# A selective-scan layer on one Trainium2 core: the copy of dt*u one group sooner, other buffer counts, and halo copies on another engine

## The chip, the core and the metric

The kernel runs on one core of a Trainium2 chip. A core has TensorE (PE in the profile; PEld is its weight load), VectorE (DVE), ScalarE (ACT), GpSimd (POOL), and SyncE (SP), which issues most of the transfers. Each engine works through its own queue of instructions in order, and engines wait for each other through semaphores. SBUF is the working memory on the chip, PSUM the memory that TensorE writes. The metric is the time of one execution on the device in microseconds (us), here the median of three.

## What is computed

The reference has two layers. Layer 1 of the program (a fractional Fourier block) is not touched. Layer 2 is a state-space block on a tensor of 4 images, 192 channels and 128 x 128 positions, read as sequences of 16,384 positions:

```python
seq = (seq - mu) * rsqrt(var + eps) * ln_g + ln_b        # over 192 channels
xs, z = split(seq @ in_proj_w.T)                         # 384 channels each
u = silu(causal_conv4(xs) + conv_b)
dt, B, C = split(u @ x_proj_w.T)                         # ranks 12, 16, 16
dt = softplus(dt @ dt_proj_w.T + dt_proj_b)
# for each channel d, state s and position t
h[d,s,t] = h[d,s,t-1] * exp(dt[d,t] * A[d,s]) + (dt[d,t] * u[d,t]) * B[s,t]
y[d,t] = sum_s h[d,s,t] * C[s,t] + u[d,t] * Dp[d]
out = x + (y * silu(z)) @ out_proj_w.T
```

A group normalisation of x stands before each layer, and its statistics for layer 2 come out of layer 1.

## The kernel before

Layer 2 is the function layer1 (the code counts from zero). Positions are cut into chunks of T = 512: 32 per image, 128 in all, numbered n. The 384 channels are three tiles of 128, numbered j. The 16 states are taken in eight groups of G = 2, numbered sg. So a chunk has 24 groups, k = 8j + sg, and the main loop has 3072 positions, pos. The order of the instructions is written out by hand (a manual schedule): each engine executes its instructions in the order in which the loop emits them.

A group's own work is spread over several positions:

- inputs (L747 to L756), emitted two groups ahead: db, the product of dt\*u with B. For sg = 1, 4, 7 GpSimd computes it from SBUF (L752). For the other five VectorE does (L754), and reads dt\*u from dp, a copy in PSUM that ScalarE makes once per j (dtu_copy, L740 to L744; one buffer).
- decay (L767): da = exp(dt\*A) on ScalarE into one of three PSUM buffers, three scans ahead. Each decay is emitted right behind the scan that frees its buffer.
- scans (L769 to L791): two scans h on VectorE (L780), each followed by a decay; between the two a callable named between is called; after them the carry copy on ScalarE (L787), and the product hc of h and C on GpSimd (L789). h has three buffers.
- sums (L792), LAG = 3 groups later: eight TensorE transposes of hc that add up into py (L802); py has one PSUM buffer.
- once per j: evacuate, a ScalarE copy of py (L811) at sg = 3; turn on TensorE at sg = 4 (L817, L819); gate on VectorE at sg = 5 (L827).

Between these pieces runs front, a generator that prepares the chunk after next: at every position the loop takes one step of it. It goes through the channel normalisation (L603 to L648), the input projection (L654), the xs activations (L667), the convolution (L672), two Silu steps (L680, L684; each loads another activation table and then the one for exp again), the projection px (L710), its copy xd, which goes to HBM as dbc and comes back broadcast as bc (L735), Softplus (L726), and dt\*u (L730, GpSimd). A front starts at k = 18 of chunk n for chunk n+2 and ends at k = 20 of chunk n+1. Where it yields LATE, the part after the yield is emitted in the same position, but behind the scans. In its middle lies this chain, one step per position: sum of squares (PE), square root (ACT), reciprocal (DVE, L634, late at k = 0), transpose into rt (PE, L637, k = 1), rows (ACT, L640, late at k = 1), broadcast by four selecting matmuls (PE, L644, k = 2), and s \*= that (DVE, L648, late at k = 2). The first input projection follows at k = 3. All of the front's and the turn's PSUM tiles are one pool, ps, of three buffers. finish (L829 to L846) is a generator, too: it projects a whole chunk back (L836, at k = 8 and 9 of the next chunk) and adds the residual on VectorE (L841, late).

The convolution reaches three positions back. A chunk's first three columns of xs are copied from halo (L663), and its last three are copied into halo (L668), both on GpSimd.

In the loop body the order of emission is: a step of finish; turn; sums of the group three back; dtu_copy for the group two on, if that begins a new j (sg = 6); at sg = 3 of every j the evacuation, which is handed to scans as the callable between, except at k = 19, where Softplus comes and the evacuation is emitted ahead of it; a step of the front; inputs; gate; scans; the late parts.

Of the kernel before, what the change touches and what calls it, by code (L numbers as in the profile page):

```python
# [10 lines left out]
F32 = mybir.dt.float32  # L11
# [18 lines left out]
T = 512  # L30
# [11 lines left out]
def _bc(ap, axis, n):  # L42

    a = ap.unsqueeze(axis)
    shape = list(a.shape)
    shape[axis] = n
    return a.to_broadcast(shape)
# [455 lines left out]
def layer1(tc, xmid, out, st2, w, n_tok=S * S):  # L503

    nc = tc.nc
    B = len(xmid)
    NCHUNK = n_tok // T
    G = 2
    LAG, FRONT, BCL = 3, 18, 5
    SOFTPLUS = 19  # L510
    LATE = True
    with ExitStack() as ctx:
        def pool(name, bufs, **kw):
            return ctx.enter_context(tc.tile_pool(name=name, bufs=bufs, **kw))
# [8 lines left out]
        scp = pool("l1s", 4)  # L523
# [53 lines left out]
        halo = cp.tile([128, NJ, 3], F32, name="halo")  # L577
# [6 lines left out]
        NG = NS // G  # L584
# [3 lines left out]
        def load_x(i):  # L588
            b, ch = divmod(i, NCHUNK)
            xm = xp.tile([CH, 2, T], F32, name="xm")  # L590
            nc.sync.dma_start(
                out=xm, in_=xmid[b][:, ch * T : (ch + 1) * T].rearrange("(t p) f -> p t f", p=CH)
            )
            got[i]["xm"] = xm

        def front(i):
# [15 lines left out]
            yield  # L612
            yield LATE
            nc.vector.scalar_tensor_tensor(
# [17 lines left out]
            nc.scalar.activation(rs, var[:, 0:4], AF.Sqrt, bias=eps, scale=1.0 / C)  # L632
            yield LATE
            nc.vector.reciprocal(rs, rs)  # L634
            yield
            rt = psum()
            nc.tensor.transpose(rt[0:4, 0:128], rs, ident)  # L637
            yield LATE
            rows = tp.tile([4, 128], F32, name="rows")
            nc.scalar.copy(rows, rt[0:4, 0:128])  # L640
            yield
# [1 line left out]
            for q in range(4):  # L643
                nc.tensor.matmul(  # L644
                    rb[0:CH, q * 128 : (q + 1) * 128], sel[:, q, :], rows, start=True, stop=True
                )
            yield LATE
            nc.vector.tensor_tensor(s, s, _bc(rb[0:CH], 1, 2), ALU.mult)  # L648
# [10 lines left out]
            xs = lp.tile([128, NJ, T + 3], F32, name="xs")  # L659
            if ch == 0:  # L660
                nc.gpsimd.memset(xs[:, :, 0:3], 0.0)
            else:
                nc.gpsimd.tensor_copy(xs[:, :, 0:3], halo)  # L663
            for j in range(NJ):
                pp = in_proj(j)
                yield
                nc.scalar.activation(xs[:, j, 3:], pp, AF.Identity, bias=bxz[:, j : j + 1])  # L667
            nc.gpsimd.tensor_copy(halo, xs[:, :, T : T + 3])  # L668

            def conv(j, pc, half):  # L670
                for k in (2 * half, 2 * half + 1):
# [60 lines left out]
        def load_bc(i, sg):  # L732

            t = bcp.tile([128, 2, G, T], F32, name="bc")
            nc.sync.dma_start(  # L735
                out=t, in_=got[i]["dbc"][:, sg * G : (sg + 1) * G, :].partition_broadcast(128)
            )
            got[i]["bc", sg] = t

        def dtu_copy(n, j):  # L740

            g = got[n]
            g["dp"] = psd.tile([128, T], F32, name="dp")
            nc.scalar.copy(g["dp"], g["dtu"][j])  # L744

        def inputs(n, k):

            g = got[n]
            j, sg = divmod(k, NG)
            db = scp.tile([128, G, T], F32, name="db")  # L750
            if sg in (1, 4, 7):
                nc.gpsimd.tensor_tensor(db, _bc(g["dtu"][j], 1, G), g["bc", sg][:, 0], ALU.mult)  # L752
            else:
                nc.vector.tensor_tensor(db, _bc(g["dp"], 1, G), g["bc", sg][:, 0], ALU.mult)  # L754
            g["db", k] = db
# [4 lines left out]
        def decay(at):  # L760

            if at < len(states):
                n, k, q = states[at]
                j, sg = divmod(k, NG)
                st = sg * G + q
                das[at] = psa.tile([128, T], F32, name="da")
                nc.scalar.activation(das[at], got[n]["dt"][j], AF.Exp, scale=A[:, j, st : st + 1])  # L767

        def scans(pos, n, k, between):  # L769
            g = got[n]  # L770
            j, sg = divmod(k, NG)
            ch = n % NCHUNK
            if k == 0:
                g["carry"] = tp.tile([128, NJ, NS], F32, name="carry")
                g["before"], last["carry"] = last.get("carry"), g["carry"]
            db = g.pop(("db", k))
            h = scp.tile([128, G, T], F32, name="h", bufs=3)
            for q in range(G):
                st = sg * G + q
                nc.vector.tensor_tensor_scan(  # L780
                    h[:, q, :], das.pop(G * pos + q), db[:, q, :],
                    0.0 if ch == 0 else g["before"][:, j, st : st + 1], ALU.mult, ALU.add,
                )
                decay(G * pos + q + 3)
                if q == 0:
                    between()
            nc.scalar.copy(g["carry"][:, j, sg * G : (sg + 1) * G], h[:, :, T - 1])  # L787
            hc = scp.tile([128, G, T], F32, name="hc")
            nc.gpsimd.tensor_tensor(hc, h, g["bc", sg][:, 1], ALU.mult)  # L789
            g["hc", k] = hc  # L790

# [16 lines left out]
        def evacuate(n, j):  # L808
            g = got[n]
            yt = g["yt", j] = op.tile([128, T // 128, 128], F32, name="yt")  # L810
            nc.scalar.copy(yt, g["py", j])  # L811
# [17 lines left out]
        def finish(n):  # L829
# [3 lines left out]
            for t in range(2):  # L833
                po = psum()
                for j in range(NJ):
# [3 lines left out]
                    )  # L839
                yield LATE  # L840
                nc.vector.tensor_add(xm[:, t, :], po[0:CH], xm[:, t, :])  # L841
# [7 lines left out]
        order = [(n, k) for n in range(total) for k in range(NGR)]  # L849
        fronts = []  # L850
# [2 lines left out]
            if n < total:  # L853
                fronts.append(front(n))

        def step(works):

            late = []
            for f in list(works):
                got_on = next(f, f)  # L860
                if got_on is f:
                    works.remove(f)
                elif got_on is LATE:
                    late.append(f)
            return late

        with tc.manual_schedule():
            for i in range(min(2, total)):
                load_x(i)
            for _ in front(0):  # L870
                pass
            for sg in range(NG):
                load_bc(0, sg)
            dtu_copy(0, 0)
            for pos in range(2):
                inputs(*order[pos])
            for at in range(3):
                decay(at)


            start_front(1)
            for _ in range(NGR - FRONT):
                for f in step(fronts):
                    next(f)
            tails = []
            for pos, (n, k) in enumerate(order):
                j, sg = divmod(k, NG)
                if k == FRONT:
                    start_front(n + 2)
                if k == NGR - 3 and n + 1 < total:  # L890
                    assert len(fronts) == (n + 2 < total), fronts
                late = step(tails)
                if pos >= NG and sg == LAG + 1:
                    turn(*before)
                if pos >= LAG and sg != LAG:
                    sums(*order[pos - LAG])
                if sg == NG - 2 and pos + 2 < len(order):
                    m, q = order[pos + 2]
                    dtu_copy(m, q // NG)
                if pos >= NG and sg == LAG:  # L900

                    before = n - (j == 0), (j - 1) % NJ
                    if k == SOFTPLUS:
                        evacuate(*before)
                late += step(fronts)
                if pos + 2 < len(order):
                    inputs(*order[pos + 2])
                if pos >= NG and sg == LAG + 2:
                    gate(*before)
                if pos >= NG and sg == LAG and k != SOFTPLUS:  # L910
                    scans(pos, n, k, lambda: evacuate(*before))
                else:
                    scans(pos, n, k, lambda: None)
                for f in late:
                    next(f, None)
                if pos >= LAG and sg == LAG:
                    sums(*order[pos - LAG])
                if k == NG - 1 and n:
                    tails.append(finish(n - 1))
                if k == FRONT - 6 and n + 2 < total:  # L920
                    load_x(n + 2)
                if k >= NGR - BCL and n + 1 < total:
                    load_bc(n + 1, k - (NGR - BCL))
                if k < NG - BCL and n:
                    load_bc(n, k + BCL)
            for at in order[-LAG:]:
                sums(*at)
            evacuate(total - 1, NJ - 1)
            turn(total - 1, NJ - 1)
            gate(total - 1, NJ - 1)  # L930
            for _ in finish(total - 1):
                pass
# [139 lines left out]
```

## Time and profile before

The time is 12446.84 us, median of three runs (12438.11 to 12448.03). The profiled run took 12437.32 us; its span is 12435.5 us. Layer 2 begins near 1500 us and fills the rest.

| engine | busy us | share of the span |
|---|---|---|
| PE (matmul) | 10160.7 | 82% |
| DVE | 11004.8 | 88% |
| ACT | 8226.0 | 66% |
| POOL | 10446.5 | 84% |

| group of instructions | count | mean ns of one |
|---|---|---|
| L789 POOL hc, 128x1024 | 3072 | 2358 |
| L752 POOL db, 128x1024 | 1152 | 2394 |
| L730 POOL dt\*u, 128x512 | 384 | 1277 |
| L780 DVE h, 128x512 | 5952 | 1263 |
| L754 DVE db, 128x1024 | 1920 | 1203 |
| L767 ACT da, 128x512 | 6144 | 688 |
| L787 ACT carry, 128x2 | 3072 | 177 |

A group's busy time is a sum over instructions, and consecutive instructions of one engine overlap a little, so the distance between their starts is shorter than their mean. In a timeline each row is a run of like instructions: start, duration of the run, engine, line, operation, operands, count, and, in brackets, how long the engine had been idle before it and what ended that wait. In the view of the waits a row is: the engine and the instruction that waited, what it waited for, the total, how many times, and the longest. Where an instruction waits for several others, the row names the one that came last by the trace, which may be another one that ended at about the same time.

### The profile page before, as it was taken

The numbers are of one execution on the slowest core, as the hardware profiler recorded it, in microseconds if no ns is written. First come the engines' busy times: TensorE is split into PE (matmuls) and PEld (weight loads), VectorE is DVE, ScalarE is ACT, GpSimd is POOL, SyncE is SP. The second block draws the span as 40 slices with busy tenths as digits, with TensorE's granted clock in tenths as the row PEclk, the third lists the DMA queues.
The fourth block names the chain that finished last, engine by engine and source line by source line (L and its number), as shares of the span: only waits on it lengthen the run. The fifth ranks groups of instructions, "written<-read, shape, count | busy, mean of one in ns | idle before, by whom it ended". The sixth has DMA issues, their size and how long they took to land.

```text
span 12435.5 us, 128056 instructions
## 1 busy us (share of the span) xinstructions
PE 10160.7 (82%) x43146; PEld 6339.5 (51%) x43146; DVE 11004.8 (88%) x10176; ACT 8226.0 (66%) x14055; POOL 10446.5 (84%) x4978
## 2 busy tenths in 40 slices
PE   4778888888888888888888888888888888888887
PEld 2434455555555555555555555555555555555554
DVE  5566599999999999999999999999999999999998
ACT  2322277777777777777777777777777777777776
POOL 0000299999999999999999999999999999999999
PEclk8888688888888888888888888888888888888888
DMA  8787532332332332332333323323323323333232
GB/s 214 210 218 200 149 117 105 107 117 97 115 117 93 117 116 96 117 110 102 117 105 107 117 98 114 117 93 117 116 96 117 111 101 117 106 106 117 98 114 89
DMA packets 503659, 1489.12 MB, mean 120 GB/s; under 512 B 67889, under 2 KB 118774, under 8 KB 502486
## 3 DMA queue, kind: packets, MB, share of 16 engines
q1 hardware_dynamic: 482518, 1418.00, 34.8%
q0 software_dynamic: 13312, 50.34, 1.3%
q10 hardware_dynamic: 7168, 12.59, 0.3%
q8 instruction: 340, 5.57, 0.2%
q14 instruction: 321, 2.63, 0.1%
HBM read 1325.19 MB, written 155.32 MB: 119 GB/s over the span
## 4 chain that ended last, share of the span: by engine, by line
DVE 47%; PE 19%; ACT 19%; issue 12%; POOL 2%; DMA 2%; SPq 0%; POOLq 0%; ACTq 0%; DVEq 0%
DVE h L780 32%; DVE db L754 11%; PE ps L654 6%; ACT da L767 6%; PE py L802 3%; ACT L767 3%; PE ps L644 2%; ACT dt L726 2%; PE pr L470 2%; ACT dp L744 1%; ACT L680 1%; ACT u L680 1%; DVE s L648 1%; ACT L726 1%; PE ps L722 1%
## 5 line engine op out<-in xcount | busy, mean ns | idle before, releaser
L789 POOL TENSOR_TENSOR hc<-h,bc 128x1024 f32<-128x1024 f32 x3072 | 7200.2, 2358 | 576.2 <-DVE h L780 415.3
L780 DVE TENSOR_TENSOR_SCAN h<-da,carry,db 128x512 f32<-128x512 f32 x5952 | 7246.0, 1263 | 218.1 <-ACT da L767 218.1
L767 ACT ACTIVATE da<-dt,c_A_log 128x512 f32<-128x512 f32 x6144 | 4171.0, 688 | 2832.5 <-DVE h L780 2815.7
L802 PE MATMUL py<-ident,hc 128*128 128x128 f32 x24576 | 3815.5, 309 | 1308.6 <-POOL hc L789 1019.8
L802 PEld LDWEIGHTS py<-ident,hc 128*128 128x128 f32 x24576 | 3320.1, 161 | 2586.0 <-issue 1363.4
L752 POOL TENSOR_TENSOR db<-dtu,bc 128x1024 f32<-128x1024 f32 x1152 | 2757.3, 2394 | 5.3 <-DMA bc<-dbc 5.3
L754 DVE TENSOR_TENSOR db<-dp,bc 128x1024 f32<-128x1024 f32 x1920 | 2310.5, 1203 | 482.3 <-ACT dp L744 445.8
L654 PE MATMUL ps<-s,c_wiT 96*128 96x512 f32 x3072 | 1689.1, 678 | 167.6 <-DVE s L648 167.6
L672 PE MATMUL ps<-xs,dcw 128*128 128x512 f32 x3072 | 1436.9, 597 | 18.0 <-ACT zs L684 0.5
L654 PEld LDWEIGHTS ps<-s,c_wiT 96*128 96x128 f32 x3072 | 586.1, 212 | 655.7 <-issue 443.6
L767 ACT ACT_TABLE_LOAD x636 | 816.0, 1283 | 11.3
L672 PEld LDWEIGHTS ps<-xs,dcw 128*128 128x128 f32 x3072 | 532.0, 190 | 480.0 <-issue 432.5
L476 POOL DMA_DIRECT2D xmid<-xt x64 | 42.6, 666 | 785.2 <-DVE xt L474 778.5
L836 PE MATMUL ps<-yg,c_woT 128*96 128x512 f32 x1536 | 700.8, 592 | 0.0
L787 ACT COPY carry<-h 128x2 f32<-128x2 f32 x3072 | 543.3, 177 | 2.6 <-DVE h L780 2.6
L817 PE MATMUL ps<-u,ddp 128*128 128x512 f32 x768 | 532.1, 782 | 0.0
L730 POOL TENSOR_TENSOR dtu<-dt,u 128x512 f32<-128x512 f32 x384 | 478.5, 1277 | 19.8 <-ACT dt L726 19.8
L191 DVE BATCH_NORM_STATS2 st<-xt 96x6 f32<-96x512 f32 x512 | 322.1, 677 | 155.3 <-DMA xt<-in_x 154.0
L836 PEld LDWEIGHTS ps<-yg,c_woT 128*96 128x96 f32 x1536 | 250.1, 163 | 400.9 <-issue 371.1
L710 PE MATMUL ps<-u,c_xpT 128*128 128x512 f32 x768 | 442.3, 719 | 0.0
L667 ACT ACTIVATE xs<-ps,bxz 128x512 f32<-128x512 f32 x384 | 264.6, 689 | 213.6 <-PE ps L654 198.9
L474 DVE TENSOR_TENSOR xt<-xt,pr 96x1024 f32<-96x1024 f32 x128 | 154.1, 1212 | 275.2 <-PE pr L470 208.8
(162 smaller groups left out, 8368.9 us busy)
## 6 DMA issues: line engine op xcount, KB each, us to landing
bc<-dbc SPq DMA_DIRECT2D x1024, 1024.0 KB, 6.7
xt<-in_x SPq DMA_DIRECT2D x192, 768.0 KB, 8.6
xmid<-xt POOLq DMA_DIRECT2D x64, 768.0 KB, 7.2
xm<-xmid SPq DMA_DIRECT2D x128, 384.0 KB, 3.3
out<-xm SPq DMA_DIRECT2D x128, 384.0 KB, 3.0
d<-x ACTq DMA_DIRECT2D x64, 192.0 KB, 7.5
df<-u SPq DMA_DIRECT2D x16, 512.0 KB, 5.0
u<-df SPq DMA_DIRECT2D x16, 512.0 KB, 11.8
```

What stands on the lines that cost most here:

```text
L654: nc.tensor.matmul(pp, wiT[:, t, m * 128 : (m + 1) * 128], s[:, t, :], start=t == 0, stop=t == 1)
L672: nc.tensor.matmul(pc, dcw[:, j, k, :], xs[:, j, k : k + T], start=k == 0, stop=k == 3)
L730: nc.gpsimd.tensor_tensor(dtu[j], dt[j], u[j], ALU.mult)
L752: nc.gpsimd.tensor_tensor(db, _bc(g["dtu"][j], 1, G), g["bc", sg][:, 0], ALU.mult)
L754: nc.vector.tensor_tensor(db, _bc(g["dp"], 1, G), g["bc", sg][:, 0], ALU.mult)
L767: nc.scalar.activation(das[at], got[n]["dt"][j], AF.Exp, scale=A[:, j, st : st + 1])
L780: nc.vector.tensor_tensor_scan(h[:, q, :], das.pop(G * pos + q), db[:, q, :], 0.0 if ch == 0 else g["before"][:, j, st : st + 1], ALU.mult ...
L787: nc.scalar.copy(g["carry"][:, j, sg * G : (sg + 1) * G], h[:, :, T - 1])
L789: nc.gpsimd.tensor_tensor(hc, h, g["bc", sg][:, 1], ALU.mult)
L802: nc.tensor.matmul(py[:, blk, :], hc[:, q, blk * 128 : (blk + 1) * 128], ident, start=first, stop=sg == NG - 1 and q == G - 1 and blk == T ...
L817: nc.tensor.matmul(pf, ddp[:, j, :], g["u"][j], start=True, stop=True)
L836: nc.tensor.matmul(po[0:CH], woT[:, j, t * CH : (t + 1) * CH], g["yg", j], start=j == 0, stop=j == NJ - 1,)
```

## The change

Four edits, all in layer 2:

1. The copy of dt\*u into dp is emitted one group sooner, at sg = 5 instead of 6. Within a chunk it stands ahead of the front's step; for the first j of the next chunk it is emitted between the two scans.
2. The rows of 1/std are copied from PSUM between the two scans of their position (that is, between two decays in ScalarE's queue) and not behind the scans.
3. The products hc have five buffers instead of four, the products db three instead of four.
4. The two halo copies go from GpSimd to ScalarE.

The purpose of 1 and 2 is to have an operand of VectorE ready sooner, of 3 to let TensorE lag further behind GpSimd at the same use of SBUF, of 4 to take work off GpSimd.

```diff
-            yield LATE
+            yield MID
             rows = tp.tile([4, 128], F32, name="rows")
             nc.scalar.copy(rows, rt[0:4, 0:128])
...
-                nc.gpsimd.tensor_copy(xs[:, :, 0:3], halo)
+                nc.scalar.copy(xs[:, :, 0:3], halo)
...
-            nc.gpsimd.tensor_copy(halo, xs[:, :, T : T + 3])
+            nc.scalar.copy(halo, xs[:, :, T : T + 3])
...
-            db = scp.tile([128, G, T], F32, name="db")
+            db = scp.tile([128, G, T], F32, name="db", bufs=3)
...
-            hc = scp.tile([128, G, T], F32, name="hc")
+            hc = scp.tile([128, G, T], F32, name="hc", bufs=5)
...
-                if sg == NG - 2 and pos + 2 < len(order):
-                    m, q = order[pos + 2]
-                    dtu_copy(m, q // NG)
-                if pos >= NG and sg == LAG:
-
+
+                new = order[pos + 3] if sg == NG - 3 and pos + 3 < len(order) else None
+                if new and new[1]:
+                    dtu_copy(new[0], new[1] // NG)
+                    new = None
+
+                done = pos >= NG and sg == LAG
+                if done:
                     before = n - (j == 0), (j - 1) % NJ
                     if k == SOFTPLUS:
                         evacuate(*before)
-                late += step(fronts)
+                        done = False
+                step(fronts, parts)
...
-                if pos >= NG and sg == LAG and k != SOFTPLUS:
-                    scans(pos, n, k, lambda: evacuate(*before))
-                else:
-                    scans(pos, n, k, lambda: None)
-                for f in late:
-                    next(f, None)
+
+                def between():
+                    if done:
+                        evacuate(*before)
+                    if new:
+                        dtu_copy(new[0], 0)
+                    go_on(parts[MID])
+
+                scans(pos, n, k, between)
+                go_on(parts[LATE])
```

More of the change, by code (lines that the diff above doesn't have):

```diff
@@ L510, in layer1 @@
     SOFTPLUS = 19
-    LATE = True
+    MID, LATE = "mid", "late"
     with ExitStack() as ctx:
@@ L854, in start_front, with step @@
                 fronts.append(front(n))
-        def step(works):
-            late = []
+        def step(works, parts):
             for f in list(works):
@@ L862, in step, with go_on @@
                     works.remove(f)
-                elif got_on is LATE:
-                    late.append(f)
-            return late
+                elif got_on is not None:
+                    parts[got_on].append(f)
+        def go_on(fs):
+            for f in fs:
+                next(f, None)
         with tc.manual_schedule():
@@ L882, in layer1 @@
             for _ in range(NGR - FRONT):
-                for f in step(fronts):
-                    next(f)
+                parts = {MID: [], LATE: []}
+                step(fronts, parts)
+                go_on(parts[MID] + parts[LATE])
             tails = []
@@ L891, in layer1 @@
                     assert len(fronts) == (n + 2 < total), fronts
-                late = step(tails)
+                parts = {MID: [], LATE: []}
+                step(tails, parts)
                 if pos >= NG and sg == LAG + 1:
@@ L904, in layer1 @@
                         evacuate(*before)
-                late += step(fronts)
+                        done = False
+                step(fronts, parts)
                 if pos + 2 < len(order):
```

## The prediction

> **What bounds the kernel now.** I read the busy time of the steady part first, then the waits of VectorE and GpSimd, then the timelines of DVE, POOL and PE over one chunk. Numbers k = 0..23 are the groups of a chunk; E(k) is the end of its scans on DVE, H(k) the end of its hc product on POOL. Busy time per engine over 10,000 us of layer 2 (columns: stretch, length, busy and count per engine, granted clock, DMA share, GB/s):
>
> ```profile
> 2000.00:12000.00 10000.00, 8325.53 (x36455) 5292.90 (x36453) 9290.78 (x8322) 7207.74 (x12423) 9475.54 (x4455) 0.86 0.32 109
> ```
>
> No engine is full, and two are close: POOL 94.8%, DVE 92.9%. One chunk takes 85.33 us: the normalisation L648 starts at 6032.27 and, 35 chunks later, at 9018.93, and 2986.66 / 35 = 85.333. So per chunk DVE works 79.3 and waits 6.05; POOL works 80.9 and waits 4.5. The waits of DVE, then of POOL, in the same stretch (117 chunks; total, times, longest):
>
> ```profile
> DVE db L754 <- ACT dp L744: 408.6, 352, 2.2
> DVE h L780 <- ACT da L767: 211.3, 235, 1.9
> DVE s L648 <- PE ps L644: 88.5, 117, 0.9
> ```
> ```profile
> POOL hc L789 <- DVE h L780: 373.9, 459, 1.3
> POOL hc L789 <- PE py L802: 146.5, 118, 2.0
> ```
>
> Per chunk DVE waits 3.5 us for the copy of dt*u, 1.8 for decays, 0.76 for the 1/std rows. The change aims at the first and third. What will they uncover? The DVE timeline of one chunk (start, us, engine, line, ..., idle before in brackets), at k = 2 to 3, 6, 9 and 14:
>
> ```profile
> 6032.27 1.22 DVE L648 TENSOR_TENSOR s<-s,ps 96x1024 f32<-96x1024 f32 x1 [0.76 <-PE ps L644]
> ...
> 6045.27 1.22 DVE L754 TENSOR_TENSOR db<-dp,bc 128x1024 f32<-128x1024 f32 x1 [1.86 <-ACT dp L744]
> ...
> 6058.70 0.69 DVE L841 TENSOR_TENSOR xm<-ps,xm 96x512 f32<-96x512 f32 x1
> ...
> 6073.33 1.22 DVE L754 TENSOR_TENSOR db<-dp,bc 128x1024 f32<-128x1024 f32 x1 [1.36 <-ACT dp L744]
> ```
>
> The PE timeline, from the last sums of the old chunk to the second output projection:
>
> ```profile
> 6028.04 1.90 PE L802 MATMUL py<-ident,hc 128*128 128x128 f32 x8 [1.93 <-POOL hc L789]
> 6030.22 2.02 PE L644 MATMUL ps<-rows,sel 4*96 4x128 f32 x8 [0.28 <-ACT rows L640]
> 6033.55 3.78 PE L654 MATMUL ps<-s,c_wiT 96*128 96x512 f32 x4 [1.31 <-DVE s L648]
> ...
> 6055.93 2.74 PE L836 MATMUL ps<-yg,c_woT 128*96 128x512 f32 x6
> 6058.50 1.04 PE L802 MATMUL py<-ident,hc 128*128 128x128 f32 x8
> ```
>
> Two things are to be seen. From 6033.55 PE shows no idle time to speak of until 6077.4: it is the busy engine of that stretch although it is at 83% overall. And L836 ends at 6055.93 + 2.74 = 6058.67, when the DVE addition that reads it starts at 6058.70 just as its scans end: no wait is recorded there, but there is no slack either. Last, POOL:
>
> ```profile
> 6025.61 6.99 POOL L789 TENSOR_TENSOR hc<-h,bc 128x1024 f32<-128x1024 f32 x3
> ...
> 6068.89 2.36 POOL L789 TENSOR_TENSOR hc<-h,bc 128x1024 f32<-128x1024 f32 x1 [0.58 <-DVE h L780]
> 6071.21 2.41 POOL L752 TENSOR_TENSOR db<-dtu,bc 128x1024 f32<-128x1024 f32 x1
> 6073.58 2.36 POOL L789 TENSOR_TENSOR hc<-h,bc 128x1024 f32<-128x1024 f32 x1
> 6077.09 2.34 POOL L789 TENSOR_TENSOR hc<-h,bc 128x1024 f32<-128x1024 f32 x1 [1.15 <-DVE h L780]
> ```
>
> After 6077.09 (k = 14) POOL never waits until the next chunk's k = 4: it is behind DVE there, and hc(23), the first of the three at 6025.61, ends at 6027.94, 5.9 us after its scans.
>
> [...] four input-projection matmuls take 3.78 us at 6033.55 and 1.88 later. [...]
>
> **The change part by part** (time 0 is the start of L648, trace 6032.27).
>
> *dt\*u copy sooner, k = 5.* ACT copies right after carry(4), ahead of the xs activation that waits for PE until 10.5. It is done near 9.5, and DVE's db at E(5) = 11.03 no longer waits: −1.86, and some 0.08 of scan start-up that each idle gap costs (a pair of scans is 2.36 start to start, 2.45 alone). DVE's own work after E(5) is 3.48 (db 1.12 and scans), 2.36, 3.48, 4.08 (with an addition of 0.6) for k = 6 to 9, so it could be at E(9) at 24.4 instead of 26.43. But L836 is at the end of PE's unbroken run, which starts 1.28 after L648. Only PE's one gap in it can close: the conv at 6054.11 waits about 0.3 for the z buffers that ACT frees, and ACT is 2 us earlier now. So L836 ends at 26.1, DVE waits about 0.5 at the first addition and 1.2 at the second, and its lead over the kernel before is 26.43 − 26.1 = 0.3 us. Of 1.94, 0.3 is left.
>
> *k = 13.* The copy comes after carry(12), while ACT is catching up with the two Silu table loads: the copy ends at 39.27, the scans at E(13) = 39.3. Wait gone, at most 0.05 left. E(14) falls from 44.6 to 42.8. POOL, which idled 1.15 before hc(14), now runs hc(12), db, hc(13), hc(14) without a gap: hc(14) starts at 43.30 instead of 44.82 (0.33 + 1.15 earlier), and from there POOL sets the pace to H(23), 36.2 us on: 79.5.
>
> *k = 21, next chunk.* The copy sits between the two scans; dtu[0] is ready at H(19) + 1.25 = 63.1 and ACT gets there at 64.9. The 0.25 us wait goes, but DVE isn't the late one there: nothing.
>
> *1/std rows between two decays.* In the trace the copy starts at 6029.92, behind the second decay; the first decay of that group ends at 6028.72, and the copy would start there, 1.2 us sooner. But the matmuls L644 also stand behind the sums of hc(23) in PE's queue, so they can't start before H(23) + 0.1 + 1.90. In the trace: 6029.98 instead of 6030.22. Gain 0.25; the L648 wait doesn't vanish. After the change L648 starts at H(23) + 4.06 (0.1, 1.90, 2.02, two hand-overs) = 79.5 + 4.06 = 83.55, whereas DVE is there at 82.5: from E(14) to E(23) it takes 30.5 today, 30.3 without the 0.25 wait at k = 22, so E(23) = 73.1, and 9.4 more to E(2) (6022.06 to 6031.45): its wait grows from 0.76 to about 1.05.
>
> *Buffers.* POOL's wait for PE py, 1.25 per chunk, is hc(6) at 6049.00. The scans of group 6 end at 6048.78, and every hc that waits for scans starts 0.22 to 0.25 after them (6068.64 to 6068.89). So the scans release it; sums(2), which frees the buffer, ended at 6043.6. A fifth buffer for C products buys nothing. Three for B products cost nothing: db(k+2) on POOL follows hc(k−1), which had waited for scans(k−1) anyway, and DVE follows itself.
>
> *Halo copies.* POOL loses two copies of 0.15 us start to start, both before a wait for DVE (hc(4), hc(6)): nothing. ACT gains two; [...] the carry copy of 2 measures 177. They lie after xs activations; the decay behind the second is ready at 14.5 and wanted at 15.7. Hidden under ACT's waits for DVE (2560.7 us in the same stretch, 21.9 per chunk). They add no foreign wait.
>
> **Sum.** Per chunk 0.3 (what PE leaves of k = 6) + 1.2 (k = 14, through POOL) + 0.25 (rows) = 1.77; 85.33 → 83.55. Times 127 chunk distances = 225 us; 12446.84 − 225 = 12222. [...] I take 12225.
>
> **Rivals.** (1) *The waits simply vanish.* For it: they are on DVE, the first engine in the chain of waits at 47%. DVE's period would be 85.33 − 3.5 − 0.76 − 0.4 (start-ups) = 80.7, POOL's floor 80.9 − 0.3 = 80.6: 81 us, 11,900. Against: L836 without slack, sums(23) ahead of L644. A half form, where [...] the k = 9 wait disappears, gives 82: 12,020. (2) *PE keeps the period.* [...] 85.33, about 12,447. [...] (3) *ACT becomes the late one.* The rows copy now waits for a PE transpose with a decay behind it, and the k = 21 copy waits for POOL. If POOL's lag eats the slack (2.5 and 1.8 us), decays are late and DVE and POOL wait: 0.6 us per chunk gives 12,525. Against: those slacks.
>
> **How the numbers follow.** Main case 0.69 (83.2 to 84.2: 12,180 to 12,310); rival 1 with its half form 0.18; rival 2 0.06; rival 3 0.07. The range from 12,030 to 12,330 holds the main case and the half form, and leaves out the full form, 2 and 3. Faster by over 0.2% is the main case and rival 1: 0.87; same 0.06; slower 0.07.
>
> **What would show it.** DVE waits for dp gone; new waits of xm L841 for PE L836 of some 1.5 us per chunk; the wait of L648 at about 1 rather than 0.76, released by PE with PE waiting for hc before it; POOL's py wait relabelled or gone, its halo copies gone; the wait for a decay at k = 20 unchanged at 1.6. No wait at L841 would make me wrong toward 11,900; waits of decays behind rows or dp toward slower.

## The result, and the profile after

The changed kernel takes 12333.99 us (median of four runs, 12330.82 to 12339.48), against 12446.15 for the kernel before: a ratio of 0.9912, with a 95% interval of 0.9894 to 0.9929. It is faster by under 1%, clear of the noise, and by about half of what was forecast (12225); the time lies 4 us above the upper end of the forecast range (12,330).

The steady part of layer 2, as a busy time per engine over 10,000 us of the kernel after (stretch, length, busy and count for PE, PEld, DVE, ACT, POOL, granted clock, DMA share, GB/s):

```profile
2000.00:12000.00 10000.00, 8362.49 (x36805) 5238.58 (x36806) 9526.04 (x8407) 7321.74 (x12786) 9540.85 (x4267) 0.84 0.32 111
```

DVE is at 95.3% now, where it was at 92.9%. The chunk period has fallen from 85.33 to 84.45 us (from the first to the last start of L730, over 127 chunks: 1506.0 to 12231.1, against 1491.1 to 12327.5). That is 0.88 less per chunk, 112 us in all. In this pair of profiled runs about 15 us go the other way before layer 2 starts (the first L730 is at 1506.0 instead of 1491.1). That part of the code is not touched by the change, and in the traces of the experiments below the first L730 lies anywhere from 1492 to 1505; the cause of this shift is open.

The waits of DVE in the kernel after, in the same stretch (119 chunks), and then those of POOL:

```profile
DVE h L780 <- ACT da L767: 156.1, 122, 1.6
DVE xm L841 <- PE ps L836: 128.7, 206, 1.1
DVE s L648 <- PE ps L644: 74.5, 118, 1.3
DVE yg L827 <- PE ps L819: 42.6, 63, 0.8
```
```profile
POOL hc L789 <- DVE h L780: 372.5, 415, 1.6
POOL hc L789 <- PE py L802: 29.7, 31, 1.2
POOL hc L789 <- PE ps L819: 24.5, 26, 1.0
```

POOL still waits 3.1 us per chunk for DVE's scans (372.5 / 119); what is left of its waits for PE is 0.25 for the sums py and 0.2 for the projection. POOL follows DVE, as before.

All of the 408.6 us of waits for dp are gone, and two new waits have come: the additions L841 wait 1.1 us per chunk for PE's projection, and the gates L827 0.36 for PE's turn. So far this is the forecast. But the waits of DVE have fallen from 6.05 to 3.4 us per chunk, by 2.65, and the period by 0.88 only. DVE's busy time has grown by 1.2 us per chunk (9526 x 84.45 / 10,000 = 80.4 against 79.3) although it executes the same instructions. The remaining 0.6 are gaps too short for the list of waits. Where do the two come from? The timeline of DVE has the answer. First a pair of scans and the db behind it in the kernel before, then in the kernel after (start, duration, engine, line):

```profile
6004.27 2.45 DVE L780 TENSOR_TENSOR_SCAN h<-da,carry,db 128x512 f32<-128x512 f32 x2
6006.64 1.20 DVE L754 TENSOR_TENSOR db<-dp,bc 128x1024 f32<-128x1024 f32 x1
```
```profile
6057.85 2.45 DVE L780 TENSOR_TENSOR_SCAN h<-da,carry,db 128x512 f32<-128x512 f32 x2
6060.34 1.23 DVE L754 TENSOR_TENSOR db<-dp,bc 128x1024 f32<-128x1024 f32 x1
```

Before, db starts 2.37 us after the scans start, that is, 0.08 before they end: the two overlap. After, it starts 2.49 after, 0.04 behind their end, and it takes 1.23 instead of 1.20. Each db that directly follows scans (11 of 15 in a chunk) now costs 0.12 to 0.15 us more.

Is it the scans that db waits for, or does db no longer overlap anything? A db with the small reciprocal L634 between it and the scans tells, in the kernel after:

```profile
6076.41 2.45 DVE L780 TENSOR_TENSOR_SCAN h<-da,carry,db 128x512 f32<-128x512 f32 x2
6078.78 0.15 DVE L634 RECIPROCAL rs<-rs 128x4 f32<-128x4 f32 x1
6078.89 1.22 DVE L754 TENSOR_TENSOR db<-dp,bc 128x1024 f32<-128x1024 f32 x1
```

The scans end at 6078.86, and db starts 0.03 behind that, while the reciprocal still runs until 6078.93. So it is the end of the scans that holds it.

The same view, the rows of the new waits in one chunk of the kernel after:

```profile
6012.66 1.23 DVE L754 TENSOR_TENSOR db<-dp,bc 128x1024 f32<-128x1024 f32 x1
...
6022.45 0.69 DVE L841 TENSOR_TENSOR xm<-ps,xm 96x512 f32<-96x512 f32 x1 [0.23 <-PE ps L836]
...
6027.62 0.69 DVE L841 TENSOR_TENSOR xm<-ps,xm 96x512 f32<-96x512 f32 x1 [0.98 <-PE ps L836]
```

At k = 6 db doesn't wait for dp any more, and 10 and 15 us later the additions wait for L836. And PE, around the rows of 1/std in the next chunk:

```profile
6081.51 1.97 PE L802 MATMUL py<-ident,hc 128*128 128x128 f32 x8 [2.06 <-POOL hc L789]
6083.41 2.02 PE L644 MATMUL ps<-rows,sel 4*96 4x128 f32 x8
6086.74 3.78 PE L654 MATMUL ps<-s,c_wiT 96*128 96x512 f32 x4 [1.31 <-DVE s L648]
```

L644 no longer waits for the rows (0.28 us before). It follows the sums of hc(23) without a gap, and these wait for POOL, as forecast.

### The profile page after: what moved, and what is told of

It reads as the page before. It is cut to its first block, busy times and chain, and to the rows that moved or that the text cites. A ratio compares the mean times of both kernels' runs of the same rounds, so it can differ in the third digit from the quotient of the medians.

```text
span 12337.7 us, 127805 instructions
## 1 busy us (share of the span) xinstructions
PE 10127.7 (82%) x43146; PEld 6238.7 (51%) x43146; DVE 11156.9 (90%) x10176; ACT 8268.8 (67%) x14307; POOL 10410.8 (84%) x4726
## 5 line engine op out<-in xcount | busy, mean ns | idle before, releaser
L802 PE MATMUL py<-ident,hc 128*128 128x128 f32 x24576 | 3764.4, 306 | 1277.1 <-POOL hc L789 1034.1
L802 PEld LDWEIGHTS py<-ident,hc 128*128 128x128 f32 x24576 | 3228.3, 159 | 2659.2 <-POOL hc L789 1448.0
L754 DVE TENSOR_TENSOR db<-dp,bc 128x1024 f32<-128x1024 f32 x1920 | 2346.3, 1222 | 105.4 <-DMA bc<-dbc 37.2
L654 PE MATMUL ps<-s,c_wiT 96*128 96x512 f32 x3072 | 1688.9, 678 | 167.8 <-DVE s L648 167.8
L654 PEld LDWEIGHTS ps<-s,c_wiT 96*128 96x128 f32 x3072 | 586.0, 212 | 655.7 <-issue 443.2
L836 PE MATMUL ps<-yg,c_woT 128*96 128x512 f32 x1536 | 700.8, 592 | 0.0
L817 PE MATMUL ps<-u,ddp 128*128 128x512 f32 x768 | 587.5, 858 | 0.0
L730 POOL TENSOR_TENSOR dtu<-dt,u 128x512 f32<-128x512 f32 x384 | 478.4, 1276 | 54.8 <-ACT dt L726 54.8
L836 PEld LDWEIGHTS ps<-yg,c_woT 128*96 128x96 f32 x1536 | 249.9, 163 | 401.0 <-issue 399.3
L722 PE MATMUL ps<-xd,c_dtT 12*128 12x512 f32 x768 | 198.2, 856 | 307.9 <-ACT xd L713 307.9
```

Source lines behind the costliest of these rows:

```text
L654: nc.tensor.matmul(pp, wiT[:, t, m * 128 : (m + 1) * 128], s[:, t, :], start=t == 0, stop=t == 1)
L730: nc.gpsimd.tensor_tensor(dtu[j], dt[j], u[j], ALU.mult)
L802: nc.tensor.matmul(py[:, blk, :], hc[:, q, blk * 128 : (blk + 1) * 128], ident, start=first, stop=sg == NG - 1 and q == G - 1 and blk == T ...
L817: nc.tensor.matmul(pf, ddp[:, j, :], g["u"][j], start=True, stop=True)
L836: nc.tensor.matmul(po[0:CH], woT[:, j, t * CH : (t + 1) * CH], g["yg", j], start=j == 0, stop=j == NJ - 1,)
```

## The experiments

The theory after this reading is A: the third B buffer makes the shortfall. With three buffers db(k+2) overwrites the buffer of db(k−1), which the scans of group k−1, the instruction right ahead of it in DVE's own queue, have just read; so it waits for their end. With four it overwrites db(k−2), which was read a group earlier. The rivals for the shortfall: B, PE's switch to full clock (a granted clock of 0.50, then 1.00; its times stand under the chunk periods) comes later on average after the change; C, the fifth C buffer matters. ("C buffers" are those of hc, "B buffers" those of db.)

### x1: four buffers each, the other three edits kept

```diff
-            db = scp.tile([128, G, T], F32, name="db", bufs=3)
+            db = scp.tile([128, G, T], F32, name="db")
-            hc = scp.tile([128, G, T], F32, name="hc", bufs=5)
+            hc = scp.tile([128, G, T], F32, name="hc")
```

> The changed kernel with four buffers each for the C products and the B products again; its other three edits stay. Theory A (the shortfall is the third B buffer: with three, the db that follows the scans of group k-1 overwrites the db those scans read, so DVE waits for its own scans to end, 0.13 us start to start at each of some 12 db per chunk): faster than the changed kernel, with 2.36 from a pair of scans to the db behind it instead of 2.49; the chunk period falls from 84.43 toward the predicted 83.55, so 12,220 to 12,280. Rival B (the shortfall is PE, whose switch to full clock comes later on average after the change): 12,330 as the changed kernel, within 15. Rival C (the fifth C buffer was worth something): slower than 12,334.

Measured: 12233.84 us (12225.94 to 12237.28), 0.983 of before (0.9816 to 0.9845), a period of 83.69. That is 100 us less than the kernel after, and what the prediction's own sum had given for the whole change. The pair of scans and db in its DVE timeline:

```profile
6008.57 2.45 DVE L780 TENSOR_TENSOR_SCAN h<-da,carry,db 128x512 f32<-128x512 f32 x2
6010.94 1.20 DVE L754 TENSOR_TENSOR db<-dp,bc 128x1024 f32<-128x1024 f32 x1
```

2.37 and 1.20 again. Its waits of DVE (120 chunks):

```profile
DVE h L780 <- ACT da L767: 213.8, 238, 1.9
DVE xm L841 <- PE ps L836: 157.6, 189, 1.1
DVE s L648 <- PE ps L644: 126.1, 120, 1.5
DVE yg L827 <- PE ps L819: 32.8, 62, 1.0
```

L648 waits 1.05 us per chunk, the forecast's number, and the additions 1.31 (forecast 1.7).

### x2: the kernel before with only the buffer counts changed

```diff
-            db = scp.tile([128, G, T], F32, name="db")
+            db = scp.tile([128, G, T], F32, name="db", bufs=3)
-            hc = scp.tile([128, G, T], F32, name="hc")
+            hc = scp.tile([128, G, T], F32, name="hc", bufs=5)
```

> The kernel before with only the buffer counts changed (five for C products, three for B products). Theory A: slower than before; DVE's own work per chunk grows by up to 12 x 0.13 = 1.6 us, of which the waits for PE and the lag of POOL hide some, so 0.3 to 1.6 us in 127 chunks: 12,485 to 12,650. Rival B: no change, 12,446. Rival C: faster, by up to the 1.25 us per chunk that POOL is recorded as waiting for PE py: 12,290.

Measured: 12581.81 us (12578.75 to 12588.81), 1.011 of before (1.0093 to 1.0127). The edit alone makes the kernel slower by 137 us, 1.08 us per chunk. Rivals B and C both fall as causes: B foresaw no change, C a gain. (PE's switch does come later in the kernel after, as a part of the way from the buffer count to the time; see the periods below.)

### x5: the kernel after with four C buffers, three B buffers

```diff
-            hc = scp.tile([128, G, T], F32, name="hc", bufs=5)
+            hc = scp.tile([128, G, T], F32, name="hc")
```

> The changed kernel with four C buffers and three B buffers: only the fifth C buffer is taken back. Theory A (the third B buffer alone makes the shortfall, the fifth C buffer is worth nothing): 12,334 as the changed kernel, within 15. Rival (the fifth C buffer helps once the rest is faster, and hides a part of the loss): slower than 12,345, with POOL waiting for PE py again by 1 us per chunk.

Measured: 12334.13 us (12332.66 to 12338.04), against 12333.99 with five. So the fifth C buffer is worth nothing measurable, and the loss of x2 is the third B buffer's.

### x3: the kernel before with only the copy of dt\*u sooner

```diff
-                if sg == NG - 2 and pos + 2 < len(order):
-                    m, q = order[pos + 2]
-                    dtu_copy(m, q // NG)
+                new = order[pos + 3] if sg == NG - 3 and pos + 3 < len(order) else None
+                if new and new[1]:
+                    dtu_copy(new[0], new[1] // NG)
+                    new = None
...
+                    if new:
+                        dtu_copy(new[0], 0)
```

> The kernel before with only the copy of dt*u one group sooner. Prediction's sum: 0.3 (what PE leaves at k = 6) plus 1.2 (k = 14, through POOL), with L648 then held by the sums of hc(23) and not by the rows: about 83.8 per chunk, 12,225 to 12,260, and new waits of xm L841 for PE L836 of 1.5 us per chunk. If the copy's waits just vanish: 3.5 us per chunk, 12,000. If PE holds the whole period: 12,446.

Measured: 12239.04 us (12232.53 to 12246.59), 0.9836 (0.9821 to 0.985). The copy alone has the whole gain: with rows and halo copies it is 12233.84, and the two ranges overlap. L841 waits 159.9 us for L836 and L648 125.3 for L644 in its list of waits, nearly as in x1.

### x4: the kernel before with only the rows between the scans

```diff
-            yield LATE
+            yield MID
             rows = tp.tile([4, 128], F32, name="rows")
...
+                    go_on(parts[MID])
```

> The kernel before with only the 1/std rows copied between the two scans. Prediction's step: L644 is held by the sums of hc(23) right behind, so 0.25 us per chunk, 12,415. If the rows were the whole of the L648 wait: 0.76 per chunk, 12,350. If the gain at L648 is lost to PE's busy stretch behind it: 12,446.

Measured: 12440.78 us (12430.32 to 12448.05), 0.9997 (0.9989 to 1.0006): nothing. Its waits of DVE (117 chunks):

```profile
DVE db L754 <- ACT dp L744: 427.9, 352, 2.2
DVE h L780 <- ACT da L767: 211.3, 235, 1.9
DVE yg L827 <- PE ps L819: 44.9, 117, 0.8
DVE s L648 <- PE ps L644: 20.9, 40, 1.3
```

The wait of L648 fell by 67.6 us. The gates now wait 43.4 more and db 19.3 more: 62.7 of it came back as waits for what PE does behind L648. The mean period is 85.33, as before, to a hundredth. Why two changes cancel so exactly is seen in the periods (below).

### x6, x7, x8: the two waits that the forecast named as the path

If PE's stretch takes back the gain at k = 6 through the additions, it must help to let the additions wait without DVE waiting. And if the sums of hc(23) hold L644, it must help to emit it ahead of them.

x6, on x1: both projections stay where they are, each addition comes one group later.

```diff
+            po = []
...
-                po = psum()
+                po.append(psum())
...
-                        po[0:CH], woT[:, j, t * CH : (t + 1) * CH], g["yg", j],
+                        po[t][0:CH], woT[:, j, t * CH : (t + 1) * CH], g["yg", j],
...
-                yield LATE
-                nc.vector.tensor_add(xm[:, t, :], po[0:CH], xm[:, t, :])
                 if t == 0:
                     yield
+            yield LATE
+            nc.vector.tensor_add(xm[:, 0, :], po[0][0:CH], xm[:, 0, :])
+            yield
+            yield LATE
+            nc.vector.tensor_add(xm[:, 1, :], po[1][0:CH], xm[:, 1, :])
```

> Like x1_pools4 (12,234), and each residual addition L841 one group later, behind the scans of k = 9 and k = 10 instead of 8 and 9; the projections L836 stay where they are. Theory (PE's unbroken stretch takes back what the sooner copy gives at k = 6, through the additions that wait for L836): the waits of xm for PE (1.3 us per chunk in x1) go, E(12) comes 1.1 us sooner, POOL starts hc(12) 1.1 sooner and the period falls from 83.67 to about 82.6: 12,095, or up to 12,150 if the gate at k = 13 then waits for PE. Rival (POOL sets the period from start to end and the additions' waits lie in DVE's slack): 12,234.

x7, on x1:

```diff
-                if pos >= LAG and sg != LAG:
+                if pos >= LAG and sg != LAG and k != 2:
                     sums(*order[pos - LAG])
...
                 step(fronts, parts)
+                if pos >= LAG and k == 2:
+                    sums(*order[pos - LAG])
```

> Like x1_pools4 (12,234), and at k = 2 PE gets the selecting matmuls L644 ahead of the sums of hc(23). Theory (the rows of 1/std are held by those sums, which wait for POOL): the wait of s L648 for PE, 1.05 us per chunk in x1, goes, and the period falls by as much to 82.6: 12,100. Rival 1 (L644 waits for the rows themselves): 12,234. Rival 2 (a sooner L648 only has PE's half-clock stretch start sooner, and its clock switch comes when it came): half of it, 12,165.

x8 has both.

> Both edits of x6_late_adds and x7_rows_first on x1_pools4. If the two waits lie one behind the other on the path that sets the end: both gains, down to what DVE needs with its waits for decays (78.7 + 1.8 + start-ups = 80.8) or POOL (80.6), so 81.0 to 81.9 per chunk: 11,900 to 12,010. If POOL's lag or the gates take one of them back: 12,050 to 12,100.

Measured: x6 12009.61 us (12007.83 to 12014.43), x7 12005.67 (12003.28 to 12015.68), x8 12002.03 (11999.06 to 12009.72); 0.9651, 0.9648 and 0.9645 of before, each with an interval of 0.0015 either way. Either edit gains some 225 us, where 140 were expected, and both together gain no more than one. x6 keeps its wait at L648, x7 its wait at L841 (127.7 us in its list); x8 has neither, but its gates wait for PE in their place:

```profile
DVE h L780 <- ACT da L767: 191.9, 121, 1.9
DVE yg L827 <- PE ps L819: 170.9, 236, 8.4
```

That both waits lay on the path is shown by x6 and x7. For why the two gains don't add there are two candidates: the gates, which now wait 1.4 us per chunk, and the periods, which are the same in all three (next). x9 below decides between them in part.

### Chunk periods

The distance between successive starts of L614 on DVE, read off the timelines from 5000 to 6800 us, in us. The mean is that of all 20 or 21 of them; the last column is the mean divided by 3.4133 us, the beat of PE's granted clock as measured here: in the traces of the kernel before and of the kernel after, every stretch at one granted clock, 0.50 or 1.00, lasts a whole number of such beats, to the nanosecond (1071 stretches before and 603 after; the last of each trace is cut off by its end):

| kernel | successive periods | mean | beats |
|---|---|---|---|
| before | 85.33 85.34 85.33 85.33 85.34 ... | 85.33 | 25.00 |
| x4 | 85.24 85.57 85.21 85.22 85.29 85.61 ... | 85.33 | 25.00 |
| x2 | 87.28 86.31 85.85 87.26 86.31 85.83 ... | 86.50 | 25.34 |
| after | 85.08 83.55 84.43 84.84 85.11 83.51 84.45 84.95 ... | 84.49 | 24.75 |
| x1 | 84.17 83.06 84.20 84.75 83.37 84.31 83.14 84.23 83.07 84.20 ... | 83.71 | 24.52 |
| x6, x8 | 81.92 81.93 81.91 81.91 81.93 ... | 81.92 | 24.00 |
| x7 | 81.72 81.72 83.12 81.72 81.72 81.72 81.73 ... | 81.92 | 24.00 |

The kernel before repeats to two hundredths of a us, the kernel after goes round in four steps and x2 in three. x1 goes back and forth between 83.07 and 84.19 (a mean of 83.63, 24.5 beats), broken now and then by a stretch like 84.75 83.37 84.31. Three different kernels have a mean of 81.92. The means lie at whole beats (25.00 and 24.00) or near simple fractions of them (24.75, 24.52, 25.34). Where the switch falls can be seen in the busy time by stretches of the kernel before, inside PE's unbroken run (the last three numbers are the granted clock, the DMA share and GB/s):

```profile
6035.00:6038.40 3.40, 3.40 (x9) 1.57 (x8) 3.40 (x4) 2.55 (x5) 3.40 (x3) 0.50 0.00 0
6038.50:6041.90 3.40, 3.40 (x21) 2.39 (x19) 3.40 (x4) 1.50 (x3) 2.46 (x2) 1.00 0.02 5
```

The granted clock is 0.50, then 1.00: half clock up to 6038.4, full clock from 6038.5, with PE busy throughout. The four matmuls of L654 take 3.78 us at 6033.55, at 0.50, and 1.88 at 6040.85, at 1.00. If the switch comes at a fixed time, a stretch that starts d sooner does its first d at half speed, and ends d/2 sooner. A disturbance of the period is then halved in each chunk.

The traces bear the halving out. The trace keeps the time of every switch of the granted clock. In the kernel before, over the stretch of the table, it comes 6.12 us after the start of L648 in every chunk. In the kernel after it moves. In two successive chunks, whose L648 start at 6085.47 and 6170.53:

```profile
6090.70:6094.00 3.30, 3.30 (x11) 2.16 (x10) 3.11 (x3) 1.76 (x5) 2.36 (x3) 0.50 0.00 0
6094.20:6097.50 3.30, 3.30 (x21) 2.29 (x20) 2.89 (x3) 1.24 (x4) 3.30 (x2) 1.00 0.00 0
6172.60:6175.90 3.30, 3.30 (x6) 1.15 (x5) 3.27 (x4) 1.79 (x3) 3.30 (x3) 0.50 0.00 0
6176.10:6179.40 3.30, 3.30 (x23) 2.53 (x22) 3.30 (x5) 1.76 (x3) 2.37 (x2) 1.00 0.00 0
```
```profile
6104.78 2.74 PE L836 MATMUL ps<-yg,c_woT 128*96 128x512 f32 x6
6188.30 2.74 PE L836 MATMUL ps<-yg,c_woT 128*96 128x512 f32 x6
```

The switch comes 8.6 us after L648 in the first and 5.5 in the second, 3.1 sooner, and the first L836 ends 22.05 and 20.51 after it, 1.54 sooner: half. Over the whole stretch the switch comes 7.45 us after L648 on average in the kernel after and 6.74 in x1. Half of the difference, 0.35 us, is what the second L841 starts later in the kernel after (26.68 against 26.33 us after L648). So, as an estimate from these numbers, some 0.35 of the 0.79 us per chunk that the third B buffer costs there come by way of PE's clock. In x4 the switch comes 7.51 us after L648, 1.4 later than before, and L836 ends 0.7 later: the rows' gain is lost there.

### x10, x11: a pure delay, to see whether the period is held

```diff
             yield LATE
+            nc.vector.tensor_copy(rb[0:CH, 0:256], rb[0:CH, 0:256])
             nc.vector.tensor_tensor(s, s, _bc(rb[0:CH], 1, 2), ALU.mult)
```

The copy is in place; it adds time and nothing else. x10 is the kernel before with it, x11 is x8 with it.

> The kernel before with an extra copy of 256 columns of the broadcast 1/std, in place in PSUM, ahead of L648 on VectorE: about 0.4 us of pure delay per chunk on the step that releases PE's long stretch. Theory of the locked period [...]: the added time is taken out of other waits, 12,446 within 10, period 85.33. Rival (each us on that path is a us of the period): 0.4 x 127 = 50 more, 12,495.

> x8_both (12,002) with the same delay of about 0.4 us ahead of L648. Locked period: 12,002 within 10, 81.92 per chunk. Rival: 12,050.

Measured: the delay is 0.46 us, from the start of the copy to that of the product:

```profile
6056.11 0.43 DVE L648 COPY ps<-ps 96x256 f32<-96x256 f32 x1 [0.75 <-PE ps L644]
6056.57 1.22 DVE L649 TENSOR_TENSOR s<-s,ps 96x1024 f32<-96x1024 f32 x1
```

x10: 12485.78 us (12476.81 to 12488.13), 1.0033 of before (1.002 to 1.0046), 45 us slower: the expectation of a held period failed for the mean, and the rival's 12,495 is nearer. But its periods are not evenly longer, as the rival has it: 87.01, 86.18, 85.77, 85.57, 85.44, 85.39, 85.37, 85.34, 85.34, 85.33, and then 87.02 again. Their distances from 85.33 are 1.68, 0.85, 0.44, 0.24, 0.11, 0.06: halved each time, until the chunk misses a switch and starts over: the switch comes 5.19 us after the start of the product in the last chunk of one round and 8.59 in the next, 3.40 later, one beat. So with the delay the period comes down to 85.33 us, 25 beats, and does not stay there. x11: 12011.18 us (12009.2 to 12015.37); 21 successive periods of 81.91 to 81.93. There the delay costs no period at all; its time is 9 us above x8, where an unheld period would have cost 58. The switch comes 6.81 us after the start of the product in x11, 7.72 in x8: the product lies 0.91 us later against it, twice the delay; half of that, by the halving above, is what PE gains back, an estimate. The waits of the gates fall from 170.9 to 119.1 us.

### x9: the gates between the scans

On x8, so that PE's turn has a scan more time:

```diff
-                if pos >= NG and sg == LAG + 2:
-                    gate(*before)
+                gated = pos >= NG and sg == LAG + 2
...
                 def between():
+                    if gated:
+                        gate(*before)
```

> Like x8_both (12,002), and the gate on VectorE, which waits 0.50 and 0.85 us for PE's turn at k = 5 and 13 there, is emitted between the two scans of its group instead of ahead of them. Theory (the gates took back what x8's second edit gave, and POOL at 98.2% leaves 80.4 us per chunk): the gate waits go, the period leaves 81.92 and lands between 80.6 and 81.1: 11,840 to 11,900. Rival [...]: 12,002, with other waits in place of the gates'.

Measured: 11859.0 us (11857.16 to 11859.82), 0.953 of before (0.9514 to 0.9546), the fastest of all, 475 us faster than the changed kernel. The waits of the gates fall from 170.9 to 17.2 us, the period leaves 81.92 and goes round in three steps, 80.93, 80.71, 80.70 (mean 80.78, 23.67 beats). So the rival, a period held at 81.92 us (24 beats) whatever DVE saves, falls: in x8 the gates' waits had kept it there. Its busy times:

```profile
2000.00:11800.00 9800.00, 8442.12 (x37690) 5359.41 (x37688) 9572.18 (x8617) 7470.81 (x13086) 9758.15 (x4372) 0.85 0.34 115
```

POOL is at 9758.15 of 9800 us, 99.6%: here POOL, whose floor the prediction put at 80.6 us per chunk, is the bound at last.

## Why the prediction was wrong

The mechanism was right in its largest parts. One sentence, a cost put at nothing, makes almost all of the miss; a second term put at nothing, the drift of PE's switch, was wrong too.

- **Failed: "Three for B products cost nothing: ... and DVE follows itself."** DVE does run them one behind the other, but here the instruction that overwrites what the one right ahead of it reads waits for that one to end (it starts 0.04 us behind that end). The overlap of scans and db is lost: start to start 2.49 instead of 2.37, and 0.03 more for db. For the 11 db per chunk that follow scans directly this is up to 1.65 us of DVE time. What remains of it on the clock is 1.08 us per chunk alone (x2) and 0.79 beside the other edits (x1 against after). x5 ascribes it to the B buffers alone. 100 of the 109 us between forecast and result are this, by x1 against after.
- **Failed: the drift of PE's switch, put at nothing.** That was the author's estimate. In the kernel before the switch comes 4.85 us into L654 (6.12 us after L648, less 1.27); in the kernel after it comes 4.2 to 7.4 into it (5.45 to 8.71 after L648), on average 1.3 later than before. Half of that, 0.65 us, is by the halving above what L836 ends later for it, an estimate; in x1 it is 0.3.
- **Right: k = 6.** The additions wait for L836: 1.1 us per chunk after, 1.31 in x1. Their waits did take back the gain: x6 removes them alone and gains 224 us. Even the 0.3 us that were to be left are 0.1 in x1 and gone in the kernel after: the second addition starts 26.33 and 26.68 us after L648, 26.43 before.
- **Right: k = 13 and 21, and POOL's lag.** No wait for dp is left. The wait of L648 grew as the sum said, to 1.05 in x1; after, with a slower DVE, it is 0.63. L644 has lost its wait for rows, and x7 shows that the sums of hc(23) held it. On average hc(23) ends 79.7 us after L648 in x1, where 79.5 was forecast and the kernel before has 81.1, and the next L648 starts 4.0 later (forecast 4.06); in the kernel after it ends at 80.5.
- **Wrong by its size: the rows, 0.25 us.** They are worth nothing (x4). The gain at L648 came back at the gates and dp, behind PE's stretch.
- **Right: fifth C buffer.** x5: 0.1 us.
- **Halo copies.** They were not taken alone; x1 and x3 differ by the rows and the halo copies together, and their ranges overlap. On ACT the two copies take 0.20 us each.
- **Right with x1, in part by luck: the sum.** 83.55 per chunk was forecast for the four edits; 83.69 is measured without the third edit, 12225 forecast, 12234 measured. But the terms (which add up to 1.75, not 1.77) err against each other: the copy alone gave 1.6 us per chunk (x3), not 1.5, and the rows 0, not 0.25.
- **Rivals.** Rival 1 (81, everything vanishes) did not come, and x6 to x9 show what it would have taken. Rival 2, whose weight of 0.06 was the author's estimate, had hold of something real: the mean period lies at 24.75 beats of PE's clock in the kernel after, where it lay at 25.00 before. Rival 3 did not come: DVE's waits for decays fell from 1.8 to 1.3 us per chunk.

What is measured for a held period: the periods of the kernel before repeat to two hundredths (85.33 and 85.34), three kernels share one mean (81.92), a disturbance is halved per chunk (1.68, 0.85, 0.44 in x10), and L836 moves by half of what PE's switch moves in the same trace (1.54 of 3.1 us). That PE's switch holds the period is inferred from these together; no run here took the half-clock stretch away. Why the kernel after settles at 24.75 beats, and x1 near 24.5, stays open.

## What to carry to other kernels

A buffer count sets how far back an instruction's overwrite reaches, on its own engine too: with one buffer fewer the writer can land on what the instruction directly ahead of it reads, and here the overlap of the two was lost with that (2.49 us from start to start instead of 2.37), at a gap too short to be seen in a list of waits. Compare start-to-start distances, not only waits. When a wait is removed, look for the next instruction that another engine finishes only just in time (a wait of zero with no slack), and when a period repeats exactly, ask what holds it before adding up gains.

## What the runs showed that was not expected

- Overlap on VectorE is worth 0.12 us per pair: 2.37 against 2.49 us from a pair of 128x512 scans to the product behind it.
- The chunk period came out at or close to 25, 24.75, 24.5 and 24 beats of PE's granted clock (3.4133 us in the traces). 0.46 us of delay in each chunk costs 45 us in all in one kernel and 9 in another.
- Two edits that each gain some 225 us gain 232 together: the gates wait for PE in place of what both removed, and only x9, which moves the gates, gains more.
